# A four-layer graph network on one core: layer 1's dense layer from eight block products to seven

## The chip, the core and the metric

The kernel runs on one core of one Trainium2 chip. The metric is the device time of one execution in microseconds (us). The engines named here are TensorE (PE, matrix products; PEld is its loading of stationary operands), VectorE (DVE), ScalarE (ACT), GpSimd (POOL) and SyncE (SP, which issues the transfers).

## What is computed

There are 32 graphs of 512 nodes with 256 features, `x`, and a dense 512 by 512 matrix `adj` each. All is float32. Four layers follow each other, and after each one the result is added to `x` and normalised over its 256 features. Cut to what matters:

```python
# layer 0:  h = (1 + eps) * x + adj @ x;  f = relu(h @ W1 + b1) @ W2 + b2        (W1 256x512, W2 512x256)
# layer 1:  h = adj @ (x @ W.T + b);      f = where(h > 0, h, alpha * h)         (W 256x256)
# layer 2:  h = layer_norm(x);            f = x + relu((adj @ h) @ W_rel + b_rel + h @ W_root)
# layer 3:  h = (eps * x + adj @ x) @ W1 + b1;  f = silu(rmsnorm(h)) @ W2 + b2   (W1 256x1024, W2 1024x256)
# after each: x = layernorm(x + f)
```

Layer 1 is the one that the change touches. The kernel computes it as `(adj @ x) @ W.T + b * rowsum(adj)`: the matrix product with `adj` first, then the small dense layer, and the bias times the row sums of `adj`.

## The kernel before

**Products by seven.** A product of two matrices, each cut into two by two blocks, can be made from seven block products in place of eight, if sums and differences of blocks are formed first and the results are added up in a certain way. `seven` (line 651) writes the order of these products and of the emptying of their three PSUM banks; `left_sums` and `right_sums` (669, 677) form the operands, four subtractions or additions each. Weights are combined once, at the start (`weight_sums`, 685, tiles named A...). All four products with `adj` (`aggregate`, 767), both dense layers of layer 0, that of layer 2 and both of layer 3 are made in this way. `dense_add` (850) is the form for a dense layer whose result is added to a tile `x` that lies by token: each of the seven products is written to PSUM in blocks of 128 columns, and DVE adds each bank to its block of `x`. Its right operands come from `dense_sums` (839), which here takes pairs of 128-row chunks.

**Layer 1's dense layer** (`layer1`, 1059; `dense_tok`, 795) is the one that is not made so. For each half of the tokens a PSUM bank takes four products of 128 by 128 with 128 by 256, eight per graph. DVE's scalar_tensor_tensor then makes `b_1 * rs + ps` for each of the four chunks of tokens (line 1071), where `rs` holds the row sums of `adj`. Then follow the leaky rectifier (ACT makes the negative part, DVE two more operations per half), and the first part of the norm.

**The norm** takes two totals over each chunk of 256 features on ACT, of the values and of their squared differences (`Norm.half`, 908, by `total`, 548). An activation with an accumulator writes a full result as well, which nobody reads. It goes to one of two constant tiles in turn, `scrap0` and `scrap1` (643); the instruction that reads the accumulator follows as an instruction of its own in the profile.

**Order of work.** The program is written out as a list of operations, and a planner (`Plan`, 221) decides in which order each engine issues them, by a list schedule over estimated times. Every operation has a rank: its graph's number times a period, less or more according to how much PE work of its graph lies ahead of it (`needs`, 324, weighted by a pace). Among the operations that an engine could start, the one of lowest rank goes first. So several graphs are worked on at once, each some way behind the one before it. `RULES` (95) lists (period, pace, spacing of the last graphs, weight); the planner makes the order for each rule and keeps the one that its estimates say ends first, which for this kernel is (42, 2, 10, 0.5). The order is then fixed: each engine takes its instructions strictly one after the other, with semaphores between engines. Up to 5 graphs are in flight. They share 36 rooms of 1024 floats per partition, halves of which can be taken (`short`), 8 PSUM banks, and 11 tiles for small vectors. Transfers are issued on SP.

**The start.** Weights and biases are loaded while graph 0 begins. For layer 2 the norm's gain and shift are folded into its weights (`fold_norm`, 1024): a row of `be_2 @ W` is made on PE, copied to a constant tile by ACT, and for one of the two weights DVE adds the bias `b_2`, which has a tile of its own.

All operations are recorded by one helper, so nearly every line of the profile says L298; groups are told apart by their tiles: `room` for the shared rooms, `ps` for PSUM, `few` for small vectors, `A` for the combined weights, and `L_gnn_W`, `L_gnn_b` and so on for those of the layers, with the layer's number left out.

Of the kernel before, what the change touches and what calls it, by code (L numbers as in the profile page):

```python
# [11 lines left out]
AF = mybir.ActivationFunctionType  # L12
ALU = mybir.AluOpType

P = 128
# [5 lines left out]
def span(ap):  # L21

    n = 1
    for d in ap.shape[1:]:
        n *= d
    return n
# [5 lines left out]
def matmul_time(n):  # L32
    return (0.223 if n <= 128 else 0.003 + n * 0.00167), 0.163
# [58 lines left out]

RULES = [(42, 2, 10, 0.5), (42, 2, 16, 0.5)]


class Pool:
# [122 lines left out]
class Plan:  # L221
# [126 lines left out]
    def best(self):  # L348


        rule = min(RULES, key=lambda rule: self.order(*rule)[0])
        return self.order(*rule)[1]
# [109 lines left out]
def tile_gnn_stack(ctx: ExitStack, tc: tile.TileContext, a: dict, out: bass.AP):  # L462
# [21 lines left out]

    nc = tc.nc
    B, N, D = a["x"].shape
    NC = N // P  # L490
    DC = D // P
# [4 lines left out]
    HC = NC // 2  # L496
    TH = N // 2
# [7 lines left out]
    plan = Plan(nc, FLIGHT)  # L505
# [24 lines left out]
    def vector(method, n, *args, **kw):  # L530
        return "vector", method, vector_time(n), args, kw

    def scalar(func, n, x, times=scalar_time, **kw):
        columns = sum(k in ("scale", "bias") and not isinstance(v, float) for k, v in kw.items())
        return "scalar", "activation", times(n, columns), (x,), dict(func=func, **kw)

    def mm(o, lhsT, rhs, first, last):
        kw = dict(start=first, stop=last, skip_group_check=True)
        way = "tensor", "matmul", matmul_time(rhs.shape[-1]), (lhsT, rhs), kw
        plan.do(o, way, ordered=o.room)  # L540
# [4 lines left out]
    def act(o, x, func, **kw):  # L545
        plan.do(o, scalar(func, span(o), x, **kw))

    def total(o, x, func, **kw):
        plan.do(o, scalar(func, span(x), x, times=total_time, **kw), scrap=next(scraps))

    def copy(o, x):
        plan.do(o, scalar(AF.Copy, span(o), x), vector("tensor_copy", span(o), x))

    def add(o, x, y):
        plan.do(o, vector("tensor_add", span(o), x, y))

    def sub(o, x, y):
        plan.do(o, vector("tensor_sub", span(o), x, y))
# [8 lines left out]
    def stt(o, x, s, y, op0, op1):  # L567
        times = (vector_time if isinstance(s, float) else columns_time)(span(o))
        way = "vector", "scalar_tensor_tensor", times, (x, s, y), dict(op0=op0, op1=op1)
        plan.do(o, way)  # L570
# [14 lines left out]
    def short(*shape):  # L585
        return Part(Room(rooms, whole=False)).shaped(*shape)

    def small(*shape):
        return Part(Room(smalls)).shaped(*shape)

    def bank(*shape):
        return Part(Room(banks)).shaped(*shape)

    def tok():
        return room(NC, D)
# [19 lines left out]
    def constant(name, shape):  # L615
        return const.tile(shape, F32, tag=name, name=name)

    def row(name):

        v = a[name]  # L620
        t = constant(name, [P, v.shape[0]])
        plan.move(t, v.partition_broadcast(P), v.shape[0] / 2)
        return t
# [8 lines left out]
    def weight(name):  # L632
        w = a[name]
        t = constant(name, [P, w.shape[0] // P, w.shape[1]])
        size = w.shape[0] * w.shape[1] / 256
        plan.move(t, w.rearrange("(c p) f -> p c f", p=P), size)
        return t
# [2 lines left out]
    ident = constant("ident", [P, P])  # L640
    make_identity(nc, ident)
    mhalf = constant("mhalf", [P, N // Q])
    scraps = [constant(f"scrap{i}", [P, D]) for i in range(2)]
    nc.vector.memset(scraps[0], 0.0)
    nc.vector.memset(mhalf, -0.5)
    pause = constant("pause", [P, 48])
    for tile_of_few in smalls.tiles:
# [29 lines left out]
    def right_sums(b11, b12, b21, b22, t, t3):  # L677

        sub(t[0], b12, b11)
        sub(t[1], b22, t[0])  # L680
        sub(t3, b22, b12)
        sub(t[2], b21, t[1])
        return dict(m1=b11, m2=b21, m3=b22, m4=t[2], m5=t[0], m6=t[1], m7=t3)

    def weight_sums(name, a11, a12, a21, a22):

        t = constant(name, [P, 3, *a11.shape[1:]])
        left = dict(m1=a11, m2=a12, m4=a22)
        left_sums(left, a21, (a21, *(t[:, i] for i in range(3))))
        return left  # L690
# [6 lines left out]
    def blocks_of(*halves):  # L697

        return (W[:, :, i * P : (i + 1) * P] for i in range(2) for W in halves)
# [92 lines left out]
        seven(*(bank(TH) for _ in range(3)), product, take, put)  # L792
        return aT

    def dense_tok(steps, h):

        ps = bank(HC, D)
        for n, (xT, W) in enumerate(steps):
            for i in range(HC):
                c = h * HC + i  # L800
                mm(
                    ps[:, i, :], xT[:, c * P : (c + 1) * P], W,
                    n == 0 and i == 0, n == len(steps) - 1,
                )
        return ps

    def dense_feat(aT, left, bias, hT, done):


# [29 lines left out]
    def dense_sums(upper, lower):  # L839


        right = {}
        for pairs in zip(upper, lower):
            blocks = [x[:, :, j * TH : (j + 1) * TH] for x in pairs for j in range(2)]
            sums = right_sums(*blocks, [short(2, TH) for _ in range(3)], blocks[1])
            for m, x in sums.items():
                right.setdefault(m, []).extend(x[:, e, :] for e in range(2))
        return right

    def dense_add(x, right, left, done):  # L850


        def block(i, j):
            return x[:, j * HC : (j + 1) * HC, i * P : (i + 1) * P]

        def product(m, ps, first):
            n = len(right[m])
            for k in range(n):
                for i in range(HC):
                    mm(  # L860
                        ps[:, i, :], right[m][k][:, i * P : (i + 1) * P], left[m][:, k, :],
                        first and i == 0 and k == 0, k == n - 1,
                    )

        def take(ps, i, j):
            add(block(i, j), ps, block(i, j))

        def put(ps, i, j, more):
            take(ps, i, j)
            if i == 1:  # L870
                done(j)

        seven(*(bank(HC, P) for _ in range(3)), product, take, put)
# [147 lines left out]
        for h in range(2):  # L1021
            add(half(x, h), half(x, h), r.unsqueeze(1).to_broadcast([P, HC, D]))

    def fold_norm(W, name):

        ps = bank(N)[:, 0:D]
        for k in range(DC):
            mm(ps, be_2[:, k : k + 1].to_broadcast([P, P]), W[:, k, :], k == 0, k == DC - 1)
        shift = constant(name, [P, D])
        copy(shift, ps)  # L1030
        for k in range(DC):
            ts(W[:, k, :], W[:, k, :], g_2[:, k : k + 1], None, ALU.mult)
        return shift


    def load_x(b):
# [22 lines left out]
    def layer1(x, adjacency):  # L1059

        rows = adjacency.row_sums()
        aT = aggregate(x, adjacency)
        rs = small(NC)
        by_token(rs, column_sums(rows), 1.0, None, ALU.mult)
        v, neg = tok(), tok()
        norm = Norm(v)
        for h in range(2):
            ps = dense_tok([(aT[:, k, :], W_1[:, k, :]) for k in range(DC)], h)
            for i in range(HC):
                c = h * HC + i  # L1070
                stt(v[:, c, :], b_1, rs[:, c : c + 1], ps[:, i, :], ALU.mult, ALU.add)
            act(half(neg, h), half(v, h), AF.Relu, scale=-1.0)
            stt(half(x, h), half(neg, h), nalpha, half(x, h), ALU.mult, ALU.add)
            stt(half(v, h), half(v, h), 0.0, half(x, h), ALU.max, ALU.add)
            norm.half(h)

        norm.scales((1.0 + LN_EPS, LN_EPS * LN_EPS), (0.25, 0.25 * LN_EPS))
        h = norm.scaled(0)
        xx = norm.scaled(1)
        u = tok()  # L1080
        for c in range(NC):
            stt(u[:, c, :], shift_rel, rs[:, c : c + 1], shift_2, ALU.mult, ALU.add)
        return h, xx, u
# [55 lines left out]


    plan.graph = -1
    idle, zeros = bank(D), scraps[0]
    for _ in range(9):
        mm(idle, zeros[:, 0:P], zeros, True, True)
    eps0 = row("L0_gnn_eps")
    one_eps0 = constant("one_eps0", [P, 1])
    ts(one_eps0, eps0, 1.0, None, ALU.add)
    loop0 = constant("loop0", [P, P])
    ts(loop0, ident, one_eps0, None, ALU.mult)
    plan.graph = 0  # L1150
    scraps = cycle(scraps)
    x = load_x(0)
    adjacency = Adjacency(0)
    W1_0 = weight("L0_gnn_W1")
# [6 lines left out]
    nalpha = constant("nalpha", [P, 1])  # L1161
    ts(nalpha, alpha, -1.0, None, ALU.mult)
    W_1 = weight("L1_gnn_W")
    b_1 = row("L1_gnn_b")
    x = layer0(x, adjacency)
    Wrel = weight("L2_gnn_W_rel")
    Wroot = weight("L2_gnn_W_root")
    b_2 = row("L2_gnn_b_rel")
    g_2 = col("L2_gnn_ln_gamma")
    be_2 = col("L2_gnn_ln_beta")  # L1170
    shift_rel = fold_norm(Wrel, "shift_rel")
    shift_2 = fold_norm(Wroot, "shift_2")
    add(shift_2, shift_2, b_2)
    A_2 = weight_sums("A_2", *blocks_of(Wroot, Wrel))
    h = layer1(x, adjacency)
    W1_3 = weight("L3_gnn_W1")
# [10 lines left out]
    for b in range(1, B):  # L1187
        plan.graph = b
        x, adjacency = load_x(b), Adjacency(b)
        h = layer1(layer0(x, adjacency), adjacency)  # L1190
# [45 lines left out]
```

## Time and profile before

| what | value |
|---|---|
| median of 3 runs | 2318.61 us (2318.61 to 2320.24) |
| the profiled execution | 2319.3 us, of which the span from first to last instruction is 2317.5 |
| granted TensorE clock | 0.999 |
| busy from 0 to 180 us: PE, DVE, ACT | 169.85, 165.45, 109.59 us |
| busy from 180 to 300 us: PE, DVE, ACT | 119.49, 110.79, 82.33 us |
| busy from 300 to 1900 us: PE, DVE, ACT | 1600.00, 1467.59, 1157.32 us |
| busy from 1900 to 2200 us: PE, DVE, ACT | 298.27, 274.33, 208.74 us |
| busy from 2200 us to the end: PE, DVE, ACT | 107.86, 101.89, 84.61 us |
| layer 1's scalar_tensor_tensor on DVE, 128x256 | x128, mean 467 ns |
| DVE additions from PSUM, 128x256 | x1056, mean 410 ns |
| DVE operations between rooms, 128x256, two groups | x448 each, mean 411 and 411 ns |
| ACT totals, 128x256 | x504 at 411 ns, x504 at 499 ns, and x1008 accumulator reads at 189 ns |

In a line of a group stand the line, the engine, the operation, the tile written and the tiles read, the shape, and the count; then the busy time in us and the mean time of one in ns; then the idle time of the engine ahead of these instructions and who ended most of it. Instructions of one engine overlap by their pipelines: the mean of one is longer than the distance from its start to the next start, and where an engine runs without a break the distance between starts is what counts. Each float32 product appears as two matmul records and two weight loads. The profile's first operand of a matmul is the moving one.

### The profile page before, as it was taken

The page shows a single profiled execution, that of the slowest core. Times are in us where ns is not written, and L with a number is a line of the kernel's source. Part 1 is how long each engine was busy: PE and PEld are TensorE (multiplying, and loading weights), DVE is VectorE, ACT ScalarE, POOL GpSimd, SP SyncE. Part 2 cuts the span into 40 slices and gives each one's busy share as a digit, 9 for nine tenths or more (in the row PEclk, how much of TensorE's full clock was granted, in tenths as well). Part 3 has the DMA queues.
Part 4 walks back from the last instruction along what each step waited for, and adds up shares of the span by engine and source line. Part 5 has one row for each costly group of instructions (what it writes and reads, how often), then busy time and mean ns, then how long its engine had stood idle before and what let it go on. Part 6 is the DMA issues. An engine that isn't in the chain of part 4 may idle for free.

```text
span 2317.5 us, 41158 instructions
## 1 busy us (share of the span) xinstructions
PE 2295.5 (99%) x14002; PEld 2089.9 (90%) x14002; DVE 2120.0 (91%) x5428; ACT 1642.6 (71%) x4444; POOL 256.9 (11%) x167
## 2 busy tenths in 40 slices
PE   9999999999999999999999999999999999999998
PEld 7889899999999999999999999999999999998988
DVE  8989999999899999999999999989999899989897
ACT  4676677776776776777767776767677677676776
POOL 0000001101101101011011111010110101101110
PEclk9999999999999999999999999999999999999999
DMA  7001222112221122211222211222112222201101
GB/s 241 21 18 19 62 58 60 24 55 62 58 60 28 54 59 65 55 43 41 56 65 57 60 25 56 61 58 59 38 46 58 65 55 52 78 13 24 55 15 42
DMA packets 223746, 122.83 MB, mean 53 GB/s; under 512 B 142896, under 2 KB 194352, under 8 KB 223536
## 3 DMA queue, kind: packets, MB, share of 16 engines
q1 hardware_dynamic: 223536, 120.20, 19.1%
q8 instruction: 111, 1.82, 0.3%
q14 instruction: 99, 0.81, 0.1%
HBM read 78.92 MB, written 24.97 MB: 45 GB/s over the span
## 4 chain that ended last, share of the span: by engine, by line
PE 89%; DVE 7%; ACT 2%; DMA 1%; issue 1%; SPq 0%; POOL 0%; ACTq 0%; DVEq 0%
PE ps L298 89%; DVE room L298 6%; ACT room L298 1%; ACT scrap L298 1%; DVE few L298 1%; DMA room<-in_x_dram 1%; DMA L_gnn_W<-in_L_gnn_W_dram 0%; DMA room<-in_adj_dram 0%; DMA L_gnn_b<-in_L_gnn_b_dram 0%; DMA diagonal<-room 0%; SPq L316 0%; ACT L298 0%; DVE A L298 0%; DVE L_gnn_W_root L298 0%; POOL few L298 0%
## 5 line engine op out<-in xcount | busy, mean ns | idle before, releaser
L298 PE MATMUL ps<-room,room 128*128 128x256 f32 x3584 | 930.9, 381 | 5.7 <-DVE room L298 3.2
L298 DVE TENSOR_TENSOR room<-room,room 128x512 f32<-128x512 f32 (+1 forms) x1360 | 773.0, 590 | 5.4 <-ACT room L298 2.8
L298 DVE TENSOR_TENSOR room<-ps,room 128x256 f32<-128x256 f32 (+1 forms) x1344 | 605.6, 469 | 143.7 <-PE ps L298 136.4
L298 PEld LDWEIGHTS ps<-room,room 128*128 128x128 f32 x3584 | 617.3, 191 | 70.3 <-DVE room L298 7.1
L298 PE MATMUL ps<-L_gnn_W,room 128*128 128x128 f32 (+1 forms) x3584 | 544.3, 290 | 1.9 <-DVE room L298 1.0
L298 PEld LDWEIGHTS ps<-L_gnn_W,room 128*128 128x128 f32 x3584 | 505.6, 191 | 33.7 <-ACT room L298 1.9
L298 PEld LDWEIGHTS ps<-A,room 128*128 128x128 f32 x3072 | 460.5, 191 | 47.3 <-DVE room L298 14.1
L298 PE MATMUL ps<-A,room 128*128 128x128 f32 x3072 | 486.9, 276 | 0.9 <-DVE room L298 0.7
L298 POOL TENSOR_TENSOR few<-few,mhalf 128x4 f32<-128x4 f32 (+2 forms) x161 | 256.2, 1598 | 2054.5 <-DVE few L298 1883.1
L298 ACT ACTIVATE room<-room,few 128x256 f32<-128x256 f32 x627 | 335.0, 596 | 159.9 <-DVE few L298 159.7
L298 PE MATMUL ps<-room,L_gnn_W 128*128 128x256 f32 x1536 | 416.4, 380 | 0.6 <-DVE room L298 0.5
L298 ACT ACTIVATE room<-ps,L_gnn_b_c 128x256 f32<-128x256 f32 x768 | 311.0, 476 | 122.3 <-PE ps L298 117.9
L298 DVE TENSOR_TENSOR room<-room 128x256 f32<-128x256 f32 (+1 forms) x640 | 308.7, 492 | 13.9 <-ACT room L298 8.2
L298 PE MATMUL ps<-room,A 128*128 128x256 f32 x1152 | 320.0, 380 | 1.1 <-ACT room L298 0.8
L298 ACT ACTIVATE room<-room 128x1024 f32<-128x1024 f32 (+2 forms) x260 | 240.8, 939 | 87.3 <-DVE room L298 84.4
L298 PEld LDWEIGHTS ps<-room,L_gnn_W 128*128 128x128 f32 x1536 | 274.5, 191 | 30.1 <-DVE room L298 1.9
L298 ACT ACTIVATE room<-ps 128x256 f32<-128x256 f32 (+1 forms) x513 | 180.1, 373 | 153.3 <-PE ps L298 153.1
L298 ACT ACTIVATE scrap<-room,few 128x256 f32<-128x256 f32 x504 | 250.7, 499 | 39.0 <-DVE few L298 38.3
L298 ACT ACTIVATE scrap<-room 128x256 f32<-128x256 f32 x504 | 206.7, 411 | 88.3 <-DVE room L298 79.8
L298 PEld LDWEIGHTS ps<-room,A 128*128 128x128 f32 x1152 | 202.8, 191 | 22.8 <-ACT room L298 2.0
L298 ACT ACTIVATE room<-room,L_gnn_rms_weight_c 128x512 f32<-128x512 f32 x256 | 173.2, 712 | 13.1 <-DVE room L298 11.0
L298 DVE TENSOR_TENSOR room<-room,loop 128x256 f32<-128x256 f32 x256 | 101.1, 411 | 2.9 <-DMA diagonal<-room 1.8
(57 smaller groups left out, 1110.6 us busy)
## 6 DMA issues: line engine op xcount, KB each, us to landing
room<-in_adj_dram SPq DMA_DIRECT2D x128, 256.0 KB, 5.0
room<-in_x_dram SPq DMA_DIRECT2D x31, 512.0 KB, 5.9
out_dram<-room SPq DMA_DIRECT2D x31, 512.0 KB, 3.2
room<-room SPq DMA_DIRECT2D x480, 32.0 KB, 2.0
diagonal<-room SPq DMA_DIRECT2D x62, 128.0 KB, 1.8
room<-in_adj_dram SPq DMA_DIRECT2D x124, 64.0 KB, 1.9
room<-diagonal SPq DMA_DIRECT2D x62, 128.0 KB, 2.2
room<-line SPq DMA_DIRECT2D x30, 256.0 KB, 3.3
```

What stands on the lines that cost most here:

```text
L298: getattr(getattr(self.nc, engine), method)(to, *(put(x) for x in args), **kw)
```

## The change

Layer 1's dense layer is made by `dense_add`, from seven products: the upper chunk of the aggregated features and the lower one are the two rows of blocks, and `A_1` holds the combined weights. Each product has two matmuls of 128 by 128 with 128 by 128. `dense_sums` takes any number of chunks now. Before the products are added, ACT writes `b_1` times the row sum into each of the four chunks of `v` (`act(..., AF.Copy, scale=rs)`), and all seven products are then added there by DVE. The rectifier and the norm's totals run as before, for each half of the tokens when that half is complete; with `seven` both halves become complete with the last two of the seven products.

The totals' unread results go to one tile, `rest`, in place of two in turn. The bias of layer 2 is loaded straight into the tile of the shift, and DVE adds the row from PSUM to it, so the tile `b_2` and one ACT copy go. The planner has one rule, with a period of 40 for 42.

```diff
-RULES = [(42, 2, 10, 0.5), (42, 2, 16, 0.5)]
+RULES = [(40, 2, 10, 0.5)]
...
     def total(o, x, func, **kw):
-        plan.do(o, scalar(func, span(x), x, times=total_time, **kw), scrap=next(scraps))
+        plan.do(o, scalar(func, span(x), x, times=total_time, **kw), scrap=rest)
...
-    scraps = [constant(f"scrap{i}", [P, D]) for i in range(2)]
-    nc.vector.memset(scraps[0], 0.0)
+    rest = constant("rest", [P, D])
+    nc.vector.memset(rest, 0.0)
...
-    def dense_tok(steps, h):
-
-        ps = bank(HC, D)
-        for n, (xT, W) in enumerate(steps):
-            for i in range(HC):
-                c = h * HC + i
-                mm(
-                    ps[:, i, :], xT[:, c * P : (c + 1) * P], W,
-                    n == 0 and i == 0, n == len(steps) - 1,
-                )
-        return ps
-
...
             blocks = [x[:, :, j * TH : (j + 1) * TH] for x in pairs for j in range(2)]
-            sums = right_sums(*blocks, [short(2, TH) for _ in range(3)], blocks[1])
+            n = blocks[0].shape[1]
+            sums = right_sums(*blocks, [short(n, TH) for _ in range(3)], blocks[1])
             for m, x in sums.items():
-                right.setdefault(m, []).extend(x[:, e, :] for e in range(2))
+                right.setdefault(m, []).extend(x[:, e, :] for e in range(n))
...
-    def fold_norm(W, name):
+    def fold_norm(W, shift, name=None):
...
-        shift = constant(name, [P, D])
-        copy(shift, ps)
+        if name:
+            plan.move(shift, a[name].partition_broadcast(P), D / 2)
+            add(shift, ps, shift)
+        else:
+            copy(shift, ps)
         for k in range(DC):
             ts(W[:, k, :], W[:, k, :], g_2[:, k : k + 1], None, ALU.mult)
-        return shift
...
         norm = Norm(v)
-        for h in range(2):
-            ps = dense_tok([(aT[:, k, :], W_1[:, k, :]) for k in range(DC)], h)
-            for i in range(HC):
-                c = h * HC + i
-                stt(v[:, c, :], b_1, rs[:, c : c + 1], ps[:, i, :], ALU.mult, ALU.add)
+        for c in range(NC):
+            act(v[:, c, :], b_1, AF.Copy, scale=rs[:, c : c + 1])
+
+        def done(h):
             act(half(neg, h), half(v, h), AF.Relu, scale=-1.0)
             stt(half(x, h), half(neg, h), nalpha, half(x, h), ALU.mult, ALU.add)
             stt(half(v, h), half(v, h), 0.0, half(x, h), ALU.max, ALU.add)
             norm.half(h)
 
+        dense_add(v, dense_sums([aT[:, 0:1]], [aT[:, 1:2]]), A_1, done)
+
...
-    idle, zeros = bank(D), scraps[0]
+    idle = bank(D)
     for _ in range(9):
-        mm(idle, zeros[:, 0:P], zeros, True, True)
+        mm(idle, rest[:, 0:P], rest, True, True)
...
     W_1 = weight("L1_gnn_W")
+    A_1 = weight_sums("A_1", *blocks_of(W_1[:, 0:1], W_1[:, 1:2]))
     b_1 = row("L1_gnn_b")
...
-    b_2 = row("L2_gnn_b_rel")
...
-    shift_rel = fold_norm(Wrel, "shift_rel")
-    shift_2 = fold_norm(Wroot, "shift_2")
-    add(shift_2, shift_2, b_2)
+    shift_rel, shift_2 = (constant(name, [P, D]) for name in ("shift_rel", "shift_2"))
+    fold_norm(Wrel, shift_rel)
+    fold_norm(Wroot, shift_2, "L2_gnn_b_rel")
```

More of the change, by code (lines that the diff above doesn't have):

```diff
@@ L1150, in tile_gnn_stack @@
     plan.graph = 0
-    scraps = cycle(scraps)
     x = load_x(0)
```

## The prediction

> **What bounds the kernel now.** I read the page's busy shares first, then the chain that ended last, then the waits of the stretch from 300 to 1900 us, where the kernel repeats itself, then the groups by shape, and last the start times in the timeline.
>
> ```profile
> PE 2295.5 (99%) x14002; PEld 2089.9 (90%) x14002; DVE 2120.0 (91%) x5428; ACT 1642.6 (71%) x4444; POOL 256.9 (11%) x167
> ...
> PE 89%; DVE 7%; ACT 2%; DMA 1%; issue 1%; SPq 0%; POOL 0%; ACTq 0%; DVEq 0%
> ```
>
> TensorE (PE) is busy and is the chain, but VectorE (DVE) is only 8 points behind: it is the engine to watch. Busy time, engine by engine, in stretches (columns: us, then busy us of PE, PEld, DVE, ACT, POOL; clock; DMA share; GB/s):
>
> ```profile
> 0.00:180.00 180.00, 169.85 (x924) 147.15 (x925) 165.45 (x443) 109.59 (x297) 11.67 (x15) 1.00 0.30 90
> ...
> 300.00:1900.00 1600.00, 1600.00 (x9775) 1461.28 (x9774) 1467.59 (x3727) 1157.32 (x3146) 185.18 (x112) 1.00 0.20 54
> ...
> 2200.00:2317.50 117.50, 107.86 (x743) 100.08 (x741) 101.89 (x247) 84.61 (x203) 13.78 (x10) 0.98 0.07 28
> ```
>
> In the middle PE has no hole. Layer 1's DVE group comes back every 71.16 us (starts at 1078.8 and 1149.9), so the stretch holds 22.5 graphs; DVE works 1467.6 / 22.5 = 65.3 us per graph and idles 5.9. The waits of that stretch (us in total, times, longest) say what the idling is:
>
> ```profile
> DVE room L298 <- PE ps L298: 109.7, 92, 2.7
> ...
> PEld ps L298 <- DVE room L298: 11.4, 44, 0.3
> ```
>
> DVE waits for PE 4.9 us per graph; PE's loads wait for DVE two times per graph, 0.3 us at most. PE sets the pace, and DVE's results come early enough, some of them only just. At the ends it is otherwise: the first 180 us have 10.1 us of PE idle with DVE at 92%; the last 117 us another 9.6.
>
> What the change touches, by shape, and the start times that give its pace (start us, us, engine, operation, count):
>
> ```profile
> L298 PE MATMUL ps<-L_gnn_W,room 128*128 128x256 f32 x512 | 143.9, 380 | 0.0
> ...
> L298 DVE SCALAR_TENSOR_TENSOR room<-L_gnn_b,few,ps 128x256 f32<-128x256 f32 x128 | 55.2, 467 | 1.5 <-PE ps L298 1.5
> ```
>
> ```profile
> 1200.78 1.89 PE L298 MATMUL ps<-room,room 128*128 128x256 f32 x8
> 1202.50 1.05 PE L298 MATMUL ps<-L_gnn_W_root,room 128*128 128x128 f32 x8
> 1203.41 1.13 PE L298 MATMUL ps<-room,room 128*128 128x256 f32 x4
> ```
>
> Each f32 product is two records (512 = 32 graphs x 8 products x 2). A record's 380 ns is latency; what counts is start to start: 8 of 256 columns take 1.72 us, 0.215 each, and 8 of 128 columns 0.91 us, 0.114. Over all records the medians are 216 and 112 ns.
>
> **What the Trainium skill says.** "TensorE: Matmul & The Clock Gate", section LDWEIGHTS: a weight load takes its columns / 1.2, so 107 ns for 128. The trace's 109 to 112 ns per 128-column record agrees: there the load, not the stream, fills the time, so halving the columns cannot go below half, and every product added pays its own load. "Perfetto Trace Analysis", Identifying the Most-Contended Engine: matmul busy time misleads, weight-load busy is better; here PEld's 90% says the same as the start times, that PE has no slack but between 0.112 and the bare load. "VectorE: DVE Perf Modes", the perf-mode tier table: an f32 tensor_tensor runs only in the 1x mode; the trace has 334 ns start to start for 256 columns, from PSUM and from SBUF alike, so no added sum is cheap.
>
> **The change part by part**, per graph unless said.
>
> *PE.* Out: 16 records of 256 columns, 16 x 0.216 = 3.46 us. In: seven products, each two matmuls of 128 columns in two records, 28 x 0.113 (the mean with switches) = 3.16. Gain 0.30 us, bounds 0.25 (by the timeline's 0.215 and 0.114) and 0.32 (by the medians). Times 32: 9.6 us (8.0 to 10.2).
>
> *DVE.* Out: four scalar_tensor_tensor at 392 ns start to start (1149.94, 1150.33 in the trace): 1.57 us. In: four subtractions for the right operands and seven additions of PSUM blocks into v, 11 x 0.334 = 3.67 us. Net +2.1 us, times 32 +67 us: 2120 becomes 2187, 94.7% of 2309. In the middle DVE's idle falls from 5.9 us per graph to 5.9 - 2.1 - 0.3 = 3.5. Cover: that idle. If it were not there, each us is a us on PE.
>
> *ACT.* In: four copies of b_1 scaled by a row sum. The nearest row, 128x256 with one per-partition operand, starts every 357 ns from PSUM and 399 ns in the totals, so 0.38 x 4 = 1.5 us. They need only the row sums and come before any product; behind them queue PSUM copies, at 71% load. The single tile for discarded results: totals that follow each other on ACT now mostly start 93 ns after the predecessor's accumulator read began (318 of 536 pairs), or 217 ns where both share a tile (some 123 pairs). With one tile all do: 318 x 0.124 = 39 us on ACT. ACT goes to 1643 + 49 + 39 = 1731, 75%. Behind a late total stand PSUM copies, then PE, by 0.12 us: hidden by the other graphs; uncovered it would be at most 1.2 us per graph.
>
> *Latency and buffers.* Before, two banks are filled and emptied in some 2.9 us. Now three banks, and four products in a row use one of them: each about 4 x 0.113 + 0.163 for the drain + 0.41 for DVE, 1.0 us, so 4 to 5 us at best, longer behind other DVE work. Both halves of v come out at the end, so the norm starts some 3 us later. That is 15 bank-us against 6 of 8 x 71; three half rooms more are held for the same time. Cost: nothing while 3.4 graphs overlap; exposed it would be 3 us, once per end.
>
> *Start.* The four sums for A_1 (128 columns, about 0.2 us each by 334 less 128/0.96) add 0.8 us of DVE, which paces the start. The bias of layer 2 lands in its own shift tile by the same 128 KB transfer on SP, and one ACT copy (0.38) goes; nothing else on SP moves by the code. Cost 0.
>
> *Order.* The rule (42, 2, 10, 0.5) is the one the planner takes before, so only 42 becomes 40: the next graph ranks 2 earlier, which at a weight of 2 is 1 us of PE work (graphs 20 instead of 21 apart). The middle is full either way: 0. The ends have 22 us of PE idle; a different order could give or take some 6 of it. I take 0.
>
> *Ends.* Three layer 1's lie in the first 180 us (at 53.6, 90.7, 156.6): 3 x 2.1 + 0.8 = 7.1 us more on a DVE with 14.5 us idle; a third of it I let through to PE: 2.5. Of the end, where layer 1's lie at 2043, 2063, 2086 and 2204, 1.0.
>
> Sum: -9.6 + 2.5 + 1.0 = -6.1 us. The profiled execution took 2319.3 (span 2317.5 and 1.8 around it), giving 2313.2; its median stands 0.7 lower, 2318.6, giving **2312.5 us**.
>
> **Rivals.** *DVE becomes the bound (slower).* In the middle DVE must give up 2.4 of its 5.9 idle us, and 4.9 of these are waits for a product not yet done. If x us per graph land on PE, the change is 27 x (x - 0.30) for the 27 graphs away from the ends, less 1.5 for the other five, plus the 3.5 at the ends. It is slower by 4.6 us or more from x = 0.40, a fifth of the 2.1 added. With a quarter, 0.53: 27 x 0.23 + 3.5 - 1.5 = +8, 2327. If DVE's idle could not shrink at all, each graph would take 2.1 us more than before: 27 x 2.1 + 2 = +59, 2377. For it: 44 near-misses of PE behind DVE; from 60 to 120 us DVE is busy 59.2 of 60 us and PE only 57.7. Against: from 1260 to 1320 us DVE is busy 58.4 of 60 and PE all 60; PE's longest wait for DVE in the middle is 0.3.
>
> *The gain goes at the ends, or a tenth of the added DVE work lands (no change).* x = 0.21 with 5 at the ends: 27 x (-0.09) + 5 - 1.5 = +1, about 2319. For it: both ends are DVE's and have three or four layer 1's each.
>
> *A bigger gain.* The order at 40 fills 4 us of the ends' holes: 2308. Nothing in the profile speaks for or against it.
>
> **How the numbers follow.** 0.2% is 4.6 us, about what a measurement of this kernel can tell from no change. Forecast 0.46, bigger gain 0.08, no change 0.21, DVE bound 0.25. The likeliest gives 2312.5, its own range 2308 to 2316. The range takes in the full gain with a better order (2318.6 - 10.2 - 4 = 2304) and the DVE case up to x = 0.6 with 2 us more lost at the ends (+12, 2331). Faster 0.54, same 0.21, slower 0.25.
>
> **What would show it.** Right: no 256-column group with L_gnn_W moving; 14386 PE records; the 128-column L_gnn_W group at 3584 and A's at 3456; the layer 1 period at 70.9 us against 71.16; DVE near 2187 us and 94.7%; PE's waits for DVE in the middle still under 20 us; ACT near 1731 with 217 ns between totals. Wrong: a period at or over 71.2, with PE or its loads waiting for DVE room; or a middle that gains and a first 180 us or a last 117 us that loses over 6 us. A 128-column record over 120 ns start to start would undo the gain at its source.

## The result: slower by 0.8%

The changed kernel takes 2336.56 us (median of 4 runs, 2336.31 to 2340.04) against 2319.43 before: a ratio of 1.0077, 95% interval 1.0065 to 1.0089, 17 us. Forecast were 2312.5 us, and 2304 to 2331 as the range. The profiled execution has a span of 2334.5 us against 2317.5.

The page of the changed kernel, busy shares and the chain by engine:

```profile
PE 2296.9 (98%) x14386; PEld 2098.0 (90%) x14386; DVE 2196.5 (94%) x5677; ACT 1708.7 (73%) x4546; POOL 243.8 (10%) x167
...
PE 55%; DVE 37%; ACT 4%; issue 3%; DMA 1%; POOL 0%; SPq 0%; DVEq 0%; ACTq 0%
```

The counts are as the change says (14386 PE records), and DVE and ACT have about the work that was forecast (2187 and 1731). But the chain, 89% PE before, now runs through DVE for 37% of the span. The stretches (us, then busy us of PE, PEld, DVE, ACT, POOL):

```profile
0.00:180.00 180.00, 165.34 (x908) 142.75 (x909) 163.05 (x447) 114.10 (x303) 11.74 (x15) 0.99 0.30 88
180.00:300.00 120.00, 117.77 (x754) 107.55 (x752) 112.59 (x296) 75.36 (x196) 14.45 (x7) 1.00 0.16 40
300.00:1900.00 1600.00, 1593.81 (x10027) 1460.93 (x10027) 1520.26 (x3909) 1202.32 (x3217) 169.66 (x113) 1.00 0.20 52
```

PE has holes in the middle, where it had none, and 4.5 us more of them at the start. The waits from 300 to 1900 us (us in total, times, longest):

```profile
DVE room L298 <- ACT room L298: 29.7, 24, 1.3
...
DVE few L298 <- ACT rest L298: 21.8, 21, 1.0
PEld ps L298 <- DVE room L298: 18.4, 43, 0.6
...
DVE room L298 <- PE ps L298: 15.1, 23, 0.9
PEld ps L298 <- ACT room L298: 6.3, 28, 0.5
PE ps L298 <- DVE room L298: 3.6, 22, 0.3
```

DVE hardly waits for PE any more (109.7 us before, 15.1 now); it waits for ACT, once per graph at each of two places, up to 1.3 and 1.0 us. And PE's loads wait for DVE and ACT longer than before (18.4 and 6.3 us for 11.4 and 0.3). Only this last pair goes with the loss: the first part of the pattern comes with the order at 40, as `b_40` will show.

**A ruler for all runs.** Layer 1's rectifier on DVE (the group with `nalpha`) comes once per half and graph. Its first start in graph 4 marks the end of the start, that in graph 27 the end of the middle; between them lie 23 periods. With the seven products both halves end together, so the mark lies somewhat later within its layer, and a part of a later graph 4 is the mark itself. By it:

| kernel | time, us | ratio, 95% interval | graph 4 at, us | period, us | graph 27 to the end, us |
|---|---|---|---|---|---|
| before | 2319.4 | | 297.4 | 71.19 | 382.7 |
| changed | 2336.6 | 1.0077 (1.0065 to 1.0089) | 306.8 | 71.42 | 385.0 |
| b_rest | 2336.2 | 1.0072 (1.0057 to 1.0087) | 300.3 | 71.74 | 385.2 |
| b_40 | 2328.7 | 1.0040 (1.0025 to 1.0055) | 302.7 | 70.98 | 391.7 |
| a_two | 2332.5 | 1.0058 (1.0042 to 1.0075) | 305.1 | 71.42 | 382.7 |
| a_42_two | 2385.5 | 1.0283 (1.0268 to 1.0298) | 309.9 | 72.33 | 411.3 |
| a_two_cut | 2328.9 | 1.0042 (1.0027 to 1.0057) | 301.6 | 71.39 | 383.2 |
| b_load | 2383.4 | 1.0275 (1.0259 to 1.0290) | 305.5 | 73.26 | 391.0 |
| b_load_u | 2335.1 | 1.0065 (1.0048 to 1.0081) | 306.0 | 71.24 | 388.9 |
| b_alt | 2315.7 | 0.9984 (0.9977 to 0.9990) | 296.6 | 71.09 | 382.8 |
| a_44 | 2315.3 | 0.9983 (0.9976 to 0.9990) | 308.9 | 70.76 | 376.9 |
| after_44 | 2326.1 | 1.0033 (1.0021 to 1.0044) | 311.4 | 71.07 | 378.1 |
| f3_44 | 2311.9 | 0.9969 (0.9956 to 0.9981) | 303.7 | 70.85 | 378.3 |
| b_alt13 | 2311.7 | 0.9969 (0.9957 to 0.9981) | 295.7 | 71.07 | 378.6 |

Of the 17.0 us between the two profiled spans, 9.4 are lost before graph 4, 23 x 0.23 = 5.3 in the middle, and 2.3 at the end.

### The profile page after: what moved, and what is told of

Read it like the earlier page. It is cut to its first block, busy times and chain, and to the rows that moved or that the text cites. A ratio compares the mean times of both kernels' runs of the same rounds, so it can differ in the third digit from the quotient of the medians.

```text
span 2334.5 us, 42231 instructions
## 1 busy us (share of the span) xinstructions
PE 2296.9 (98%) x14386; PEld 2098.0 (90%) x14386; DVE 2196.5 (94%) x5677; ACT 1708.7 (73%) x4546; POOL 243.8 (10%) x167
## 4 chain that ended last, share of the span: by engine, by line
PE 55%; DVE 37%; ACT 4%; issue 3%; DMA 1%; POOL 0%; SPq 0%; DVEq 0%; ACTq 0%
PE ps L298 55%; DVE room L298 34%; ACT rest L298 3%; DVE few L298 3%; ACT room L298 1%; DMA room<-in_adj_dram 0%; POOL few L298 0%; DMA diagonal<-room 0%; SPq L316 0%; DVE A L298 0%; DVE pause L1188 0%; DMA room<-room 0%; DVEq L298 0%; DVE L_gnn_W L298 0%; ACTq L298 0%
## 5 line engine op out<-in xcount | busy, mean ns | idle before, releaser
L298 DVE TENSOR_TENSOR room<-ps,room 128x256 f32<-128x256 f32 (+1 forms) x1568 | 691.5, 461 | 38.0 <-PE ps L298 32.0
L298 PEld LDWEIGHTS ps<-L_gnn_W,room 128*128 128x128 f32 x3584 | 540.2, 191 | 48.7 <-ACT room L298 4.4
L298 PE MATMUL ps<-L_gnn_W,room 128*128 128x128 f32 x3584 | 564.4, 275 | 4.8 <-DVE room L298 2.7
L298 PE MATMUL ps<-A,room 128*128 128x128 f32 x3456 | 525.0, 275 | 4.2 <-DVE room L298 2.3
L298 PEld LDWEIGHTS ps<-A,room 128*128 128x128 f32 x3456 | 495.5, 191 | 34.3 <-DVE room L298 4.6
L298 ACT ACTIVATE rest<-room,few 128x256 f32<-128x256 f32 x504 | 253.8, 504 | 164.0 <-DVE few L298 158.2
L298 DVE TENSOR_TENSOR room<-room 128x256 f32<-128x256 f32 (+1 forms) x704 | 340.1, 487 | 10.2 <-ACT room L298 4.8
L298 ACT ACTIVATE rest<-room 128x256 f32<-128x256 f32 x504 | 208.0, 413 | 84.3 <-DVE room L298 74.3
L298 ACT ACTIVATE room<-ps 128x256 f32<-128x256 f32 x493 | 177.6, 373 | 94.7 <-PE ps L298 94.4
L298 DVE TENSOR_SCALAR few<-few 128x2 f32<-128x2 f32 (+3 forms) x583 | 86.9, 158 | 32.0 <-ACT rest L298 30.0
```

The costliest lines, as they stand in the source:

```text
L298: getattr(getattr(self.nc, engine), method)(to, *(put(x) for x in args), **kw)
```

## Experiments

### One part at a time

Four kernels: the changed one with two tiles for unread results again (`a_two`), this with the period 42 (`a_42_two`), and the kernel before with the single tile alone (`b_rest`) and with the period 40 alone (`b_40`).

```diff
# a_two, from the changed kernel (there is no room for a second float32 tile)
+    rest1 = const.tile([P, D], mybir.dt.bfloat16, tag="rest1", name="rest1")
+    scraps = cycle([rest, rest1])
...
-... scrap=rest)
+... scrap=next(scraps))
# a_42_two: the same, and
-RULES = [(40, 2, 10, 0.5)]
+RULES = [(42, 2, 10, 0.5)]
# b_rest, from the kernel before
-... scrap=next(scraps))
+... scrap=scraps_first)          # scraps_first = scraps[0]
# b_40, from the kernel before
-RULES = [(42, 2, 10, 0.5), (42, 2, 16, 0.5)]
+RULES = [(40, 2, 10, 0.5)]
```

> The changed kernel with a second tile for the totals' unread results again (a bfloat16 one, for room), everything else as changed. Theory T1 (the single tile makes ACT late against the plan, DVE stands behind it in order, 2.35 us per graph in the middle, and that stall is what PE sees): DVE's waits for ACT from 300 to 1900 us fall from 51 us to under 15, the period from 71.36 to under 71.1, time 2316 to 2324. Theory T2 (DVE's added 2.1 us per graph are the bound by themselves): waits for ACT fall but DVE then waits for PE, period stays at 71.3 or above, 2330 or more. Theory T3 (the order at 40): no change, 2336.

> As the run with two tiles, and the planner's period 42 again: only layer 1 by seven products, with the bias in layer 2's tile, is left of the change. T1: like the run with two tiles within 4 us. T2: 2330 or more. T3: 2312, 15 us or more below the run with two tiles and 40.

> The kernel before with one tile for all of the totals' unread results, nothing else. T1: ACT's pairs of totals go from 93 to 217 ns; DVE has 5.9 us of idle per graph here, so part of the delay is taken up: DVE's waits for ACT rise from 6 us to 20 or more in the middle, time 2320 to 2328. T2 and T3: 2319 within 3 us.

> The kernel before with the planner's one rule at 40, nothing else. T3: 2327 or more, with the loss in the first 300 us. T1 and T2: 2319 within 4 us.

*The single tile.* `b_rest` issues the same instructions in the same order as the kernel before, on every engine, and takes 16.9 us more. That is above what T1 expected. The same stretch of ACT's timeline in both (start us, us, engine, operation), first the kernel before:

```profile
1157.07 0.50 ACT L298 ACTIVATE scrap<-room,few 128x256 f32<-128x256 f32 x1
1157.46 0.19 ACT L298 ACTIVATION_READ_ACCUMULATOR scrap<-room,few 128x1 f32 x1
1157.69 0.42 ACT L298 ACTIVATE scrap<-room 128x256 f32<-128x256 f32 x1
1158.01 0.19 ACT L298 ACTIVATION_READ_ACCUMULATOR scrap<-room 128x1 f32 x1
1158.10 0.49 ACT L298 ACTIVATE scrap<-room,few 128x256 f32<-128x256 f32 x1
```

and `b_rest`:

```profile
1166.47 0.49 ACT L298 ACTIVATE scrap<-room,few 128x256 f32<-128x256 f32 x1
1166.87 0.19 ACT L298 ACTIVATION_READ_ACCUMULATOR scrap<-room,few 128x1 f32 x1
1167.09 0.42 ACT L298 ACTIVATE scrap<-room 128x256 f32<-128x256 f32 x1
1167.42 0.19 ACT L298 ACTIVATION_READ_ACCUMULATOR scrap<-room 128x1 f32 x1
1167.63 0.51 ACT L298 ACTIVATE scrap<-room,few 128x256 f32<-128x256 f32 x1
```

From the second read to the next total is 0.09 us where the tiles differ, 0.21 where they are one; where neighbours shared a tile before, as in the first pair, it was 0.23 already. These eighths of a microsecond on an engine that is busy 72% cost 0.55 us per graph in the middle. The waits of `b_rest` from 300 to 1900 us show where they come out:

```profile
PEld ps L298 <- DVE room L298: 20.8, 44, 0.6
...
DVE few L298 <- ACT scrap L298: 10.0, 22, 0.5
...
PE ps L298 <- DVE room L298: 4.4, 22, 0.2
```

A total is late, and the small DVE operation on its result stands at the head of DVE's queue for up to 0.5 us once per graph. That what is queued behind it then reaches PE late is read from these sums (20.8 us where it was 11.4), not followed instruction by instruction; DVE's idle of some 6 us per graph lies elsewhere in its queue and does not help. `a_two` against the changed kernel, the same instructions in the same order too, gives a price of only 4.0 us, at the start and the end; the runs of the two (2331.0 to 2335.3 and 2336.3 to 2340.0 us) lie so close that it is rough. The middle stays at 71.42, and so do the waits there, from 300 to 1900 us in `a_two`:

```profile
DVE room L298 <- ACT room L298: 29.7, 24, 1.3
...
PEld ps L298 <- DVE room L298: 19.8, 43, 0.8
...
DVE few L298 <- ACT rest L298: 17.5, 21, 0.8
DVE room L298 <- PE ps L298: 15.2, 23, 0.9
```

So T1 has the right mechanism for `b_rest` and fails for the changed kernel: in its middle the waits for ACT are not there because of the tile (51 us become 47). The price of the same 93 to 217 ns depends on the order. That the second tile of `a_two` is bfloat16 does not matter to ACT's pace: in `a_44` the totals that write it reach their read after 306 and 399 ns, in `b_alt` with float32 alone after 307 and 399.

*The order at 40.* `b_40` takes 9.4 us more: it is faster in the middle (70.98), and loses 5.3 us before graph 4 and 9.0 us at the end. T3 placed the loss in the first 300 us, which holds for the smaller part of it. DVE has 5631 instructions in it for 5428: 28 normalisations that ACT made before, and 174 more of the small memsets to a tile `pause` by which the planner holds DVE back (0.1 us each). Its waits from 300 to 1900 us:

```profile
DVE room L298 <- ACT room L298: 55.5, 45, 1.5
...
DVE room L298 <- PE ps L298: 16.5, 49, 0.9
...
PEld ps L298 <- DVE room L298: 4.8, 20, 0.3
```

DVE hardly waits for PE here either, and stands for ACT as long as in the changed kernel, and yet this middle is the fastest of all with eight products. What is shorter are the waits of PE's loads: 4.8 us, for 11.4 before and 19.8 in `a_two`. `a_42_two` goes the other way, and far: with the new layer 1 the period 42 is the bad one, 53 us worse than 40, and in its middle PE's loads wait 43.3 us for ACT; why that order does so I did not follow up. Neither part has a price of its own; each order is a new arrangement. From before, by way of `b_40` and `a_two`, to the changed kernel: +9.4 for the order at 40, +3.8 for the seven products in it, +4.0 for the single tile. The +3.8 hides two large parts, by the table: +2.4 before graph 4, +10.1 in the middle (23 x 0.44) and -9.0 at the end, where the loss of the order at 40 is gone again.

### Is it DVE's work?

`a_two_cut` keeps the order of `a_two` and takes 1.6 us per graph off DVE. `b_load` keeps the order of before and does layer 1's four operations on DVE twice; `b_load_u` does so with four others, elsewhere in its queue. Planned were 1.57 us more per graph. The traces show some 2.05: a repeat writes the same tile as the operation ahead of it, carries a wait for it, and starts 0.51 us after it, not 0.39. That is as much as the change adds to DVE. `b_alt` is the kernel before with every neighbouring pair of totals on different tiles, and `a_44` the seven products in another order.

```diff
# a_two_cut: issued with 2 x 16 columns, planned as before
+                    nc.vector.tensor_add(o.place(), few.place(), o.place())   # block(i, j)[:, :, 0:16], ps[:, :, 0:16]
# b_load: at layer 1's stt(v[:, c, :], b_1, rs, ps, ...), b_load_u: at stt(u[:, c, :], shift_rel, rs, shift_2, ...)
+                def issue(one=op[1]):
+                    one()
+                    one()
# b_alt: the tile is taken when the instruction is issued
-            to = put(out) if scrap is None else scrap
+            to = put(out) if scrap is None else next(scrap)
# a_44, from a_two: tiles as in b_alt, and
-RULES = [(40, 2, 10, 0.5)]
+RULES = [(44, 2, 13, 0.5)]
```

> The kernel before, same order of instructions, its two tiles for unread results now handed out in turn as the instructions are issued (before they were handed out in the order of writing, so some neighbours in ACT's queue share one). Theory U-tile (what the single tile costs is the wait of a total for the total just ahead of it): no pair at 217 ns is left, and as 318 pairs more cost 16.9 us, undoing the other 125 or so gains 2 to 6 us: 2313 to 2317. If it is not that wait: 2319 within 2 us.

> The changed kernel with two tiles, order at 40 as it was, but layer 1's seven additions from PSUM work on 32 of their 256 columns each, which takes some 7 x 0.23 = 1.6 us per graph off DVE and nothing off PE (that part of the result is left out). U-DVE (DVE's work sets the pace of the middle): the period falls from 71.36 to under 71.0 and the time to 2322 or less. U-loop (waits handed round PE, ACT and DVE in their fixed orders set it): DVE's idle grows by the 1.6 us, the period stays over 71.25, 2328 or more.

> The kernel before, same order, each of layer 1's four scalar_tensor_tensor done twice: 1.57 us more of DVE per graph, 94% in all, without any of the rest of the change. U-DVE: before has 5.9 us of idle on DVE per graph, so little is lost: period under 71.35, 2319 to 2326. U-loop: lateness against the planned order lands on PE, period 71.5 or more, 2329 or more.

> Layer 1 by seven products, two tiles in turn as issued, and the planner's rule (44, 2, 13, 0.5). If the loss of the change is the order that came with it and not the added DVE work, a period near 70.8 and a time of 2306 to 2316, below both kernels. If DVE's 94.7% cannot be had without stalls whatever the order: 2320 or more.

> The kernel before, same order, with the four scalar_tensor_tensor that make u for layer 2 done twice in place of those of layer 1: the same 1.57 us more of DVE per graph, at another place of its queue. If the amount of DVE work decides (U-DVE): as the run that doubled layer 1's four, 2383 within 5 us. If the place in the fixed order decides (U-loop): another time by 10 us or more, and if that place has slack, under 2330.

*Taking work away* gives nothing in the middle: 71.39 for 71.42. The next operation starts 107 ns after each of these additions, for 334 in `a_two`, which is the 1.6 us. Some 1.2 of it turn up as DVE's waits for PE, 15.2 us in `a_two` and the first and last of these lines in `a_two_cut`:

```profile
DVE room L298 <- PE ps L298: 32.5, 45, 0.9
...
PEld ps L298 <- DVE room L298: 18.1, 43, 0.8
...
DVE room L863 <- PE ps L298: 8.7, 23, 0.4
```

PE's waits for DVE stay (18.1; 19.8 in `a_two`). So U-DVE falls for the middle, as far as these seven additions go: their work is not what stands in line there. At the start it holds: graph 4 comes 3.5 us earlier.

*Adding work* shows the same from the other side. At layer 1's four operations, some 2.05 us per graph make the period 2.07 us longer: all that was added. At u's four about as much makes it 0.05 us longer. From 300 to 1900 us, `b_load`:

```profile
DVE room L298 <- PE ps L298: 103.9, 89, 2.7
PEld ps L298 <- ACT room L298: 52.2, 88, 1.9
...
PE ps L298 <- ACT room L298: 29.2, 22, 1.5
```

and `b_load_u`:

```profile
DVE room L298 <- PE ps L298: 66.6, 55, 2.7
...
PEld ps L298 <- DVE room L298: 12.8, 49, 0.3
...
PEld ps L298 <- ACT room L298: 0.3, 1, 0.3
```

In the second DVE's waits for PE shrink from 109.7 us to 66.6: here the idle is the cover that I had counted on. In the first they do not shrink (103.9), and PE stands instead, for ACT. One such place in `b_load`, DVE, ACT and PE's loads in turn:

```profile
1185.12 1.90 DVE L298 SCALAR_TENSOR_TENSOR room<-L_gnn_b,few,ps 128x256 f32<-128x256 f32 x4
...
1187.05 0.63 ACT L298 ACTIVATE room<-room 128x512 f32<-128x512 f32 x1 [1.27 <-DVE room L298]
...
1188.13 1.08 ACT L298 ACTIVATE room<-room,few 128x256 f32<-128x256 f32 x2
...
1188.77 0.30 PEld L298 LDWEIGHTS ps<-room,room 128*128 128x128 f32 x2 [1.74 <-ACT room L298]
```

Two of layer 1's operations and their repeats, 1.90 us for a half, are late; the rectifier on ACT stands 1.27 us for them; behind it in ACT's queue are a total and the normalisation of another graph, which has nothing to do with layer 1, and PE's next product stands 1.74 us for that. The idle time of an engine in a fixed order belongs to one place in its queue. At the start both runs lose some 8 us (305.5 and 306.0 for 297.4). Up to that mark 18 and 20 repeats have run, 9.2 and 10.3 us at 0.51 each: there, in the order of before, most of the added DVE work lands at either place. That, and 6.2 us at the end, is why `b_load_u` is not under 2330 as I expected of a place with slack.

*Another order.* `a_44` has DVE at 96% in the middle and PE without a hole:

```profile
300.00:1900.00 1600.00, 1599.51 (x10118) 1477.98 (x10118) 1533.85 (x3960) 1186.46 (x3238) 173.95 (x113) 1.00 0.20 53
```

Its period, 70.76, is 0.33 us below that of `b_alt`, about the 0.30 us that seven products should gain on PE. The two have different orders, though, and the order alone moved the period of the kernel before by 0.21 (`b_40`), so the agreement does not measure the gain. DVE at 96% is no bound by itself: in the changed kernel's middle 95% went with 71.42. `a_44` still ends level with `b_alt`, since its start takes longer: 12.3 us by the mark, 7.3 by the first product with `L_gnn_W_root` in graph 4 (354.4 for 347.1 us), which is free of the mark's own shift. `b_alt` itself is 3.5 us faster than the kernel before, by nothing but the last 217 ns pairs gone, as U-tile expected.

### How far it goes

`after_44` is the changed kernel with only the rule replaced; `f3_44` makes layer 1 by eight in graphs 0 to 2 and by seven from graph 3 on; `b_alt13` is `b_alt` with another spacing of the last graphs.

```diff
# after_44, from the changed kernel
-RULES = [(40, 2, 10, 0.5)]
+RULES = [(44, 2, 13, 0.5)]
# f3_44, from a_44
-RULES = [(44, 2, 13, 0.5)]
+RULES = [(44, 2, 8, 0.5)]
+FIRST = 3
...
+        straight = plan.graph < FIRST      # then layer 1 as in the kernel before; A_1 is made at graph 3
# b_alt13, from b_alt
-RULES = [(42, 2, 10, 0.5), (42, 2, 16, 0.5)]
+RULES = [(42, 2, 13, 0.5)]
```

> The changed kernel with nothing but its planner's rule replaced by (44, 2, 13, 0.5): the single tile stays. Beside the run at 44 with two tiles in turn (same order of instructions) it gives the price of the single tile in that order; beside the changed kernel the price of the order at 40. If the order at 40 is most of the loss: 2320 to 2328. If the single tile is: 2330 or more.

> Layer 1 by seven products from graph 3 on and by eight in graphs 0 to 2, where DVE sets the pace; two tiles in turn as issued; rule (44, 2, 8, 0.5). If the start of the run at 44 (graph 4's layer 1 at 308.9 us against 297.4 before) is lost to DVE's added work there, graph 4's layer 1 comes at 300 or earlier and the time is 2303 to 2310. If the start is lost to the order at 44 itself: 2313 or more.

> The kernel before with its two tiles in turn as issued and the one rule (42, 2, 13, 0.5), which differs from the order of before in the spacing of the last three graphs. The middle as in the run with the tiles in turn, 71.08; the end 1 to 4 us shorter: 2311 to 2316.

The order takes 10.5 us off the changed kernel (2336.6 to 2326.1), and in that order the single tile still costs 10.8 (against `a_44`, the same instructions in the same order). `f3_44` brings graph 4 5.2 us earlier than `a_44`, not the 9 or more that I expected, so part of the slow start seems to be DVE's added work and part the order at 44. The runs don't part the two cleanly, for `f3_44` is planned anew with another spacing of the last graphs. `f3_44` and `b_alt13` beat both kernels by 0.3% and are level with each other: on this kernel, with the orders tried, the seven products bring nothing that eight with well-placed tiles do not.

## Why the prediction was wrong

The measured 2336.6 us lie above the range. Three steps put a cost at nothing that was not nothing (the order, the single tile, the cover of DVE's added work), and behind them stand two readings: that an idle share is a reserve, and that a PE that is busy all the time is at its limit.

- **PE's gain: the price is right, 0.30 us per graph, but it is not seen in the changed kernel.** The matmuls of 128 columns still start every 112 ns, those of 256 every 216, and the counts of records came as forecast. A load of 107 ns was set beside those 112 ns; the loads' own records last 191 ns in the trace of before, overlapped, and half of the 216 ns for 256 columns is 108, so nothing here says which of the two fills a short record.
- **"Hidden by the other graphs", of the single tile: failed.** The time on ACT was sized rightly (93 to 217 ns), and put at nothing because ACT is at 71%. Alone it costs 16.9 us in the order before, 10.8 at 44, and about 4.0 in the change itself.
- **"The middle is full either way: 0", of the order: failed, and with it "in the middle PE has no hole".** PE is busy for all of the 1600 us in the kernel before, in `b_alt` and in `b_40`, with 436 records per graph in each, and the periods are 71.19, 71.09 and 70.98. Busy time on PE hides short waits: its loads wait for DVE 11.4, 6.1 and 4.8 us. For the ends I allowed 6 us. The order at 40 alone costs 9.4, made of -4.8 in the middle, +5.3 and +9.0 at the ends; with the new layer 1, 40 and 42 are 53 us apart.
- **"Cover: that idle", of DVE's added 2.1 us: the step that cost the middle.** In the order at 40 the seven products lengthen the period by 0.44 us, where -0.30 was forecast: 0.74 of the 2.1 reach PE. Some 2.05 us added to the kernel before cost 64 us at one place and 15 at another. Whether the idle covers depends on the place, and the prediction did not ask where it lies. Over the whole kernel the seven products, in the order at 40, cost 3.8 in place of a gain of 6.1.
- **The ends.** The 2.5 us allowed for DVE's work at the start are about what the seven products cost there (2.4, `a_two` against `b_40`), which is luck: in the order of before most of the added work lands (`b_load`, `b_load_u`). The changed kernel loses 9.4 us before graph 4, of which the order at 40 alone is 5.3 and the single tile 1.8.
- **The rival that DVE becomes the bound** has the right sign. Its formula with the x = 0.53 that the middle shows gives +8 us, half of the 17 measured. That x is the one it assumed is luck, too: it is made of -0.21 for the order and +0.44 for the products. Its mechanism is not shown: taking work off DVE at layer 1's additions leaves the period as it was. What is left is a round of waits between PE, ACT and DVE in their fixed orders, which is argued and not shown. Which wait closes it stays open. DVE's waits for ACT, the longest in the changed kernel, can't be told by their size: `b_40` has as much of them (55.5 us) at a period of 70.98.

## What to carry to other kernels

Where several engines run fixed orders near saturation, an engine's idle share is no reserve: ask at which place in its queue the idle lies, and what is queued behind the instruction that gets longer. Nor is an engine that is busy all the time at its limit: three orders of one kernel, with PE busy throughout, differ by 0.2 us per graph. A scratch output that nobody reads is a resource like any other: hand out such tiles in the order of issue, and count what the sharing adds to each pair. And a planner's parameter has no price of its own: change it alone, and again with the other edits, before any of them is blamed.

## What was not expected of the hardware

Two ACT instructions with an accumulator that write the same unread tile stand 217 ns from the first one's accumulator read to the second's start, in place of 93, though both run on one engine in order. The packed trace says what holds the second: in `b_rest` all 449 totals that follow another so closely carry a wait for the semaphore that ACT's own instructions raise, and they start some 30 ns after the read ahead of them (187 ns) has ended; at 93 ns a total starts while that read still runs. So this is a wait that the program itself carries for the shared tile, and what the engine would do without it no run shows. DVE has the like: in `b_load` an operation that repeats the one ahead of it into the same tile carries such a wait and starts 511 ns after it, where in the kernel before the next operation of the four starts after 392.

In the order of the kernel before, 318 such pairs more, some 39 us of ACT's time in all, cost 16.9 us of the kernel's, which is more than the 9.6 us that seven products for eight were to take off PE.
